# A Flamingo block's last stage: values of all head pairs two at a time, the second slot in another order

## The chip, the cores and the metric

The kernel runs on one core of a Trainium2 chip. The metric is the device time of one execution in microseconds (us). The kernel before takes 1775.0 us (median of 3 runs, 1774.93 to 1775.4). All data are float32. The core has five engines with a queue of instructions each: TensorE (PE in the profile; its weight loads are PEld), VectorE (DVE), ScalarE (ACT), GpSimd (POOL) and SyncE (SP), which here only issues DMAs. Every queue runs in order.

## The reference

Two layers of "gated cross attention, then feed forward" over 16 sequences of 256 tokens with 256 features. The change touches only the last of the four parts, a gated linear attention (GLA) with 8 heads of 64:

```python
q1 = (x @ Wq).reshape(B, L, H, DK) * scale          # keys and queries of the dense half
k1 = (x @ Wk).reshape(B, L, H, DK)
v = (x @ Wv).reshape(B, L, H, DV)
q2 = (x @ Wqa @ Wqb).reshape(B, L, H, DK) * scale    # of the sparse half
k2 = softmax((x @ Wka @ Wkb).reshape(B, L, H, DK))
gk1 = log_sigmoid(x @ Wg1a @ Wg1b + bg1) / 16        # decays
gk2 = log_sigmoid(x @ Wg2a @ Wg2b + bg2) / 16
e = softmax(x @ We);  idx = top_k(e, 1)              # each token chooses one of 4 experts
...
o = o_dense + o_sparse                               # chunked GLA, 64 tokens a chunk
g = (x @ Wga @ Wgb).reshape(B, L, H, DV)
o = o * rsqrt(mean(o * o) + EPS) * norm_w
o = o * (g * sigmoid(g))
return o.reshape(B, L, H * DV) @ Wo
```

Here `x` is the layer norm of the stream, and the result times tanh of a gate is added to the stream.

## The kernel before, in words

`stage3_fast` is the last stage. A batch is one sequence of 256 tokens, and its 8 heads are taken as 4 head pairs. Head pair p (0 to 63) belongs to batch b = p // 4, and m = p % 4 is its place in the batch. The loop `for p in range(last - 1)` runs one **slot** per head pair; a slot's number in the text is p % 4. In slot p the keys, queries and decays of head pair p+1 are made, the products of head pair p, and values of earlier head pairs.

The order of the work is written out by hand. Every instruction of this stage is tied to its place in the program, on every engine (`Pinned`, `keep_in_program_order`). The tables `middle`, `rest`, `late`, `behind_factors`, `by_rows` and `logs` give for each slot number the pieces of per-batch work to run at that point; an entry `(f, d, ...)` calls `f` for batch b + d. Waits come from the data and from buffers that are used again.

The pieces that matter here, with their names and lines:

- `keys_queries` (1861) fills one bank of PSUM, `kq`; `decays` (1869) fills `gq` and `gz` and lets ScalarE make four exponentials, `ee`; `second` (1881) puts the sparse half's queries and keys ahead into the other halves of `gq` and `gz`. `factors` (1915) multiplies `kq` by `ee` on VectorE and so frees `kq`; `factors_second` (1922) makes `k` on GpSimd and `q` on VectorE.
- `products(p, n)` (1930) makes the score products, `sc<-f` for the dense half (n = 0) and `sc<-q,k` for the sparse half (n = 1). `masked(p, n)` (1949) multiplies them by masks on VectorE, and for n = 1 GpSimd adds the two halves (`at<-at,at`).
- `values(p)` (1967) multiplies the sum by v, into the bank `o`, two head pairs to a bank. `squares` (1982 ff.) and `gated` (1991) read that bank. `summed(p)` (2110) decides which values come in which slot: both head pairs 2 and 3 of the batch before in slot 0, head pair 0 in slot 1, head pair 1 in slot 2, none in slot 3.
- `norms` (2014) makes the sums of squares (`ms`), takes them through Ln and Exp, and sends them over DRAM (`rms`, `r`) to all partitions; `normed_out` (2030) applies them on GpSimd; `project` (2035) multiplies by Wo, adds to the stream and sends out.
- `stats` (1678), `norm_ahead` (1688) and `turn_ahead` (1701) prepare the layer norm of the batch two ahead: moments on VectorE and GpSimd, the normed rows `xn` on ScalarE, and then the turn. The turn is a VectorE transpose in blocks of 32 (`turned<-xn`) and 16 DMAs on SP's queue that put the blocks into `xnT`. `bias` adds a vector to the stream ahead of stats.
- `lows` (1711) reads all of `xnT` in slot 0, for the batch one ahead. `route_logits`, `route_sums` and `route` (1735 to 1764) choose the expert; the choice goes through DRAM (`picks`) back as `rows` and `cols`. `same` (1799) and `weights` (1806) turn these into the masks `em` and `am`.
- `all_gates` (1775) makes the decays' gates: four matmuls into `sc` (two) and two rotating banks (one each), and exponentials into `lg`; the fourth exponential is put off to `gates_end`. `gate_logs` and `steepest` follow. `outgates`, `outgates_copy` and `outgates_end` (1824 to 1852) make the output gate `gw`.

PSUM has eight banks: `kq`, `gq`, `gz` and `o` one each, `sc` two, and two that rotate (`bank`).

The lines that order the values before the change:

```python
                if p % 4 == 3 and p < last - 1:
                    return
                if p % 4 == 0:
                    values(p - 2)
                values(p - 1)
                if p % 2 == 0:
                    squares((p - 1) // 4, (p - 1) % 4 // 2)
```

Of the kernel before, what the change touches and what calls it, by code (L numbers as in the profile page):

```python
# [10 lines left out]
F32 = mybir.dt.float32  # L11
I32 = mybir.dt.int32
AF = mybir.ActivationFunctionType
# [4 lines left out]
P = 128  # L18
# [55 lines left out]
def layers(ctx: ExitStack, tc: tile.TileContext, t, out, check):  # L74
# [1559 lines left out]
    def stage3_fast(early_bank):  # L1634

        with ExitStack() as sx:
# [64 lines left out]
            def turn_ahead(b):  # L1701
# [5 lines left out]
                for q in range(0, P, 32):  # L1707
                    for r in range(0, P, 32):
                        sp.dma_start(out=to[r:r + 32, :, q:q + 32], in_=y[q:q + 32, :, r:r + 32])

            def lows(b):

                low[b] = of(b).tile([P, 2, S], F32, tag="low", name="low")
                ps = bank("low")
                for c in range(2):
                    for k in range(2):
                        matmul(ps[:, c * S:(c + 1) * S], la[:, k, c * P:(c + 1) * P], xnT[b][:, k, :],
                                         start=k == 0, stop=k == 1)
# [30 lines left out]
            def route(b):  # L1749

                e, q = e_.pop(b), small("eq", few)
                w, c = choice[own_rows, :8], choice[own_rows, 8:16]
                dve.tensor_tensor(e, e, bc(den_.pop(b), few, 2), ALU.mult)
                dve.tensor_reduce(w, e, AX.X, ALU.max)
                dve.tensor_tensor(q, e, bc(w, few, 2), ALU.is_equal)
                dve.tensor_tensor(q, q, bc(prio[own_rows, 4:], few, 1), ALU.mult)
                dve.tensor_reduce(c, q, AX.X, ALU.max)
                dve.transpose(chosen[own_rows], choice[own_rows])
                sp.dma_start(out=picks[b].rearrange("n (k a) -> (n k) a", a=32), in_=chosen[64:80])
                x = w2.tile([P, 512], F32, tag="zs", name="rows") if b else w0.tile([P, 4, P], F32, tag="turned", name="rows").rearrange("p x d -> p (x d)")  # L1760
                rows[b] = x.rearrange("p (n s) -> p n s", n=2)
                sp.dma_start(out=rows[b], in_=bc(picks[b], [P, 2, S], 0))
                cols_[b] = w1.tile([P, 2, 2], F32, tag="cols", name="cols")
                sp.dma_start(out=cols_[b], in_=picks[b].rearrange("n (i p) -> p n i", p=P))
# [10 lines left out]
            def all_gates(b):  # L1775

                lg[b] = of(b).tile([P, 2, 2, 512], F32, tag="lg", name="lg")
                two = psa.tile([P, 2, 512], F32, tag="sc", name="sc")
                one = [bank("z"), bank("z")]
                for i in (1, 0):  # L1780
                    for n, (lo, hi) in enumerate(((0, 17), (32, 49))):
                        x, w = (low2[lo:hi, :], lbg2[lo:hi, :]) if i else (low[b][64 + lo:64 + hi, 1, tokens(0)],
                                                                         lbg[64 + lo:64 + hi, :])
                        matmul(two[:, n, :] if i else one[n], x, w, start=True, stop=True)
                act3.activation(lg[b][:, 0, 0, :], one[0], AF.Exp, scale=-1.0)
                act3.activation(lg[b][:, 1], two, AF.Exp, scale=-1.0)
                z_[b, "z"] = one[1]

            def gates_end(b):
                act3.activation(lg[b][:, 0, 1, :], z_.pop((b, "z")), AF.Exp, scale=-1.0)  # L1790

            def gate_logs(b, i):
                act3.activation(lg[b][:, i], lg[b][:, i], AF.Ln, bias=1.0)
# [136 lines left out]
            def products(p, n):  # L1930

                b, m, cols = place(p)
                q, k = fq.pop((p, n)), fk.pop((p, n))
                if p == last - 1 and n == 1:
                    two = [psu.tile([P, 512], F32, tag=x, name="sc1") for x in ("kq", "gq")]
                elif n == 1 and m > 1:
                    two = [bank("sc1"), bank("sc1")]
                else:
                    ps = z_[p, n, "sc"] = psa.tile([P, 2, 512], F32, tag="sc", name="sc")
                    two = [ps[:, 0, :], ps[:, 1, :]]  # L1940
                for lo, hi, i in ((0, S, 0), (P, S, 1)):
                    for j in range(2):
                        r = slice(64 * j, 64 * j + 64)
                        matmul(two[j][:, lo + i * P:hi + i * P], k[r, tokens(i)], q[r, lo:hi],
                                         start=True, stop=True)
                if n == 1:
                    z_[p, n, "sc"] = two

            def masked(p, n):
# [6 lines left out]
                else:  # L1956
# [5 lines left out]
                    if p == last - 1:  # L1962
                        at[p, 1] = a
                        return
                    pool3.tensor_tensor(at[p], at[p], a, ALU.add)

            def values(p, first=True, end=True):
                b, m, cols = place(p)
# [38 lines left out]

            rms = [tc.dram_tile([8, S], F32, name=f"rms{b}") for b in range(B - 1)]

            def scaled_first(b):  # L2010
                if b == B - 1:
                    scaled(b, 0)

            def norms(b):

                if b == B - 1:
                    return
                ps, x = bank("ms"), sq.pop(b)
                for m in range(4):
                    matmul(ps[32 * m:32 * m + 32, :S], halves[:, 48:80], x[:, m, :], start=True, stop=True)  # L2020
                y = w2.tile([P, S], F32, tag="rs", name="rs")
# [29 lines left out]
            def project_part(b, i, h):  # L2051
# [4 lines left out]
                if h == 1:  # L2056
# [4 lines left out]
            start = {}  # L2061
# [18 lines left out]
            yield  # L2080
            for group in (((stats, 0),), ((norm, 0),), ((turn, 0),), ((lows, 0),), ((gates, 0, 0), (route_logits, 0)),
                          ((route_sums, 0), (route, 0)), ((gates, 0, 1), (gate_logs, 0, 0)),
                          ((vals, 0), (gate_logs, 0, 1), (stats, 1), (steepest, 0, 0), (same, 0))):
                for f, *a in group:
                    f(*a)
                yield
# [21 lines left out]

            dve3.tensor_scalar(wo, wo3, vec[:, V_NW:V_NW + 1], None, ALU.mult)
            def summed(p):  # L2110
                if p % 4 == 3 and p < last - 1:
                    return
                if p % 4 == 0:
                    values(p - 2)
                values(p - 1)
                if p % 2 == 0:
                    squares((p - 1) // 4, (p - 1) % 4 // 2)

            for p in range(last - 1):
                run(start, p)  # L2120
# [36 lines left out]
            masked(p, 1)  # L2157
            scaled(b, 0)
            project(b - 1, 0)
            summed(p)  # L2160
            values(p, end=False)
            values(p, first=False)
            ends = Verdict()
# [138 lines left out]
```

## Time and profile before

| what | value |
|---|---|
| median of the runs | 1775.0 us (1774.93 to 1775.4) |
| profiled execution, whole | 1775.26 us |
| its span, first to last instruction | 1773.5 us |
| mean granted TensorE clock | 0.999 |
| last stage's matmuls | from 1217 us to the end |
| one batch of the last stage, 1425.10 to 1459.41 | 34.31 us: PE busy 34.31, DVE 27.07, ACT 18.96, POOL 17.72 |

In the rows of the profile a name such as `o<-at,v 128*64 128x256 f32 x16` reads: what is written, what is read, the part of TensorE's array that is used (rows*columns), the shape, the type, and how many instructions stand in the row. A timeline row begins with the start and the length of the row in us; "[0.70 <-...]" is the idle time of the engine before it, and what ended that. In the table of waits the three numbers are the total in us, how often, and the longest. Every logical float32 matmul appears as two instructions.

### The profile page before, as it was taken

Reading aid. Unit: us, or ns where it says so; the run is one execution under the profiler, and the core shown is the slowest. Engines: PE = TensorE matmul, PEld = TensorE weight load, DVE = VectorE, ACT = ScalarE, POOL = GpSimd, SP = SyncE. Lnnn points to the kernel's source line nnn. Section 1 sums busy time; section 2 is a strip of 40 time slices with the busy share of each in tenths; the row PEclk is TensorE's granted clock in tenths of the full one; section 3 lists DMA queues with packets and bytes.
Section 4 is the critical chain, followed back from the end, with each engine's and each line's share of the span. In section 5 each row is a group of like instructions: output and inputs, shape, how many; then the busy total and the mean of one; then the engine's idle time right before and its main releaser. Section 6 shows DMA issues by size and latency. Waiting matters only on the chain.

```text
span 1773.5 us, 35324 instructions
## 1 busy us (share of the span) xinstructions
PE 1753.7 (99%) x13800; PEld 1224.6 (69%) x13800; DVE 1182.6 (67%) x2713; ACT 854.6 (48%) x1764; POOL 1016.4 (57%) x1002
## 2 busy tenths in 40 slices
PE   8999999999999999999999999999999999999998
PEld 5666666666666766666678776666777777777776
DVE  3345665656566656666557358888878877877875
ACT  4434444334433443344333357886546545655653
POOL 3655676677557666677562586632544545554553
PEclk9999999999999999999999999999999999999999
DMA  9800010100100010001018883300111211211121
GB/s 309 242 1 22 14 39 7 32 20 13 32 26 20 12 36 10 29 10 35 10 56 256 248 206 49 50 14 17 32 42 36 52 42 35 51 40 42 39 45 33
DMA packets 121626, 102.31 MB, mean 58 GB/s; under 512 B 53052, under 2 KB 106980, under 8 KB 120938
## 3 DMA queue, kind: packets, MB, share of 16 engines
q1 hardware_dynamic: 109161, 83.17, 16.5%
q0 software_dynamic: 12288, 16.79, 4.7%
q8 instruction: 111, 1.82, 0.4%
q14 instruction: 66, 0.53, 0.1%
HBM read 56.26 MB, written 38.44 MB: 53 GB/s over the span
## 4 chain that ended last, share of the span: by engine, by line
PE 87%; POOL 7%; DVE 3%; issue 1%; ACT 1%; DMA 1%; SPq 0%; POOLq 0%; ACTq 0%
PE o L50 12%; PE qk L50 11%; PE v L50 9%; PE sc L50 8%; PE proj L50 8%; PE kq L1652 7%; PE sc L1652 6%; POOL es L50 4%; PE gq L1652 4%; PE v L1652 3%; PE ex L50 3%; PE proj L1652 3%; PE o L1652 3%; PE gz L1652 2%; PE q L50 2%; POOL rs L50 2%
## 5 line engine op out<-in xcount | busy, mean ns | idle before, releaser
L50 POOL TENSOR_SCALAR rs<-mv 128x2 f32<-128x2 f32 (+2 forms) x85 | 16.2, 190 | 373.1 <-DVE mv L50 366.9
L50 DVE RECIPROCAL rd<-o 128x256 f32<-128x256 f32 x64 | 112.3, 1755 | 164.2 <-PE o L50 123.8
L50 POOL TENSOR_TENSOR at<-at,at 128x768 f32<-128x768 f32 x63 | 114.3, 1814 | 144.9 <-DVE at L50 144.5
L50 ACT ACTIVATE e<-sc 128x1024 f32<-128x1024 f32 (+1 forms) x192 | 181.5, 1015 | 18.5 <-PE sc L50 18.5
L50 PE MATMUL sc<-qk 64*128 64x256 f32 (+1 forms) x1536 | 183.1, 384 | 0.5 <-DVE qk L50 0.5
L50 PE MATMUL o<-e,v 128*32 128x256 f32 (+1 forms) x3072 | 177.9, 379 | 0.0
L50 PEld LDWEIGHTS sc<-qk 64*128 64x128 f32 (+1 forms) x1536 | 132.0, 172 | 55.1 <-issue 26.8
L50 POOL TENSOR_TENSOR esum<-esum,es 128x512 f32<-128x512 f32 x128 | 163.4, 1277 | 10.0
L50 PE MATMUL qk<-kvT,wkv 128*128 128x333 f32 x512 | 164.3, 443 | 0.0
L50 ACT ACTIVATE qk<-qk 128x256 f32<-128x256 f32 x128 | 48.7, 381 | 231.8 <-PE qk L50 231.8
L50 POOL TENSOR_TENSOR es<-e 128x1024 f32<-128x1024 f32 x64 | 151.3, 2364 | 12.0 <-ACT e L50 9.0
L50 POOL TENSOR_TENSOR es<-es,e 77x1024 f32<-77x1024 f32 x64 | 150.3, 2349 | 5.0
L50 PEld LDWEIGHTS o<-e,v 128*32 128x32 f32 (+1 forms) x3072 | 99.9, 110 | 66.3
L50 PE MATMUL qk<-kvT,wq 128*128 128x256 f32 x512 | 134.6, 385 | 0.0
L50 DVE COPY qk<-qk 128x333 f32<-128x333 f32 x128 | 64.6, 504 | 93.8 <-ACT qk L50 92.8
L50 POOL DMA_INDIRECT x<-rows_out,pos x64 | 100.8, 1575 | 33.5 <-issue 15.9
L50 PEld LDWEIGHTS qk<-kvT,wq 128*128 128x128 f32 x512 | 94.2, 189 | 35.2 <-issue 9.6
L50 PEld LDWEIGHTS qk<-kvT,wkv 128*128 128x128 f32 x512 | 97.2, 190 | 30.0
L50 PE MATMUL proj<-wo0h,oT 128*128 128x256 f32 x512 | 113.7, 380 | 0.3 <-DVE oT L50 0.3
L50 PE MATMUL v<-wkv,kvT 128*128 128x512 f32 x256 | 113.1, 595 | 0.0
L50 PEld LDWEIGHTS proj<-wo0h,oT 128*128 128x128 f32 x512 | 95.9, 190 | 13.9 <-issue 0.8
L50 POOL DMA_INDIRECT rows<-xw,pos x64 | 66.7, 1041 | 57.5 <-DMA rows<-xw,pos 21.6
(256 smaller groups left out, 3912.6 us busy)
## 6 DMA issues: line engine op xcount, KB each, us to landing
rows<-zero SPq DMA_DIRECT2D x16, 640.0 KB
xin<-rows SPq DMA_DIRECT2D x16, 640.0 KB
r<-rms SPq DMA_DIRECT2D x30, 256.0 KB
rows_out<-y SPq DMA_DIRECT2D x16, 384.0 KB
v<-vctx SPq DMA_DIRECT2D x15, 308.0 KB
x<-in_x_dram SPq DMA_DIRECT2D x16, 256.0 KB
rows_out<-y SPq DMA_DIRECT2D x16, 256.0 KB
rows<-picks SPq DMA_DIRECT2D x16, 256.0 KB
```

Source lines behind the costliest of these rows:

```text
L50: x = getattr(self.engine, name)(*a, **k)
L1652: tc.keep_in_program_order(nc.tensor.matmul(*a, **k))
```

## The change

- `summed` now gives values in slots 0 and 2 only, two head pairs each time. Slot 1 has none, and its second products (n = 1) come directly behind the first, in the two rotating banks; the sum of head pair 0's halves (`both`) is put to the end of slot 1.
- The factors of the next head pair come ahead of the products in slots 1 and 62 too.
- `all_gates` makes its last exponential at once; `gates_end` goes. `norms` writes into the bank `o`.
- `outgates_end` moves from slot 1 to slot 2, `stats` from slot 1 to slot 0, `norm_ahead` from slot 2 to slot 0, `bias` from slot 0 to slot 3 of the batch before, the first `steepest` from slot 2 to slot 3.
- The turn stands behind `weights` in slot 2, except that for batch 2 it stays at the earlier place.
- `rows` lies in the tile `turned` of the first pool instead of a `zs` buffer (for batch 1 in an `sq` buffer).
- `start`, `scaled_first` and the tests for `ahead` go; the first two had no work to do.

```diff
+            def turn_in_first(b):
+                if b == 2:
+                    turn_ahead(b)
+
+            def turn_behind_first(b):
+                if b > 2:
+                    turn_ahead(b)
...
-                x = w2.tile([P, 512], F32, tag="zs", name="rows") if b else w0.tile([P, 4, P], F32, tag="turned", name="rows").rearrange("p x d -> p (x d)")
-                rows[b] = x.rearrange("p (n s) -> p n s", n=2)
+                if b == 1:
+                    rows[b] = w2.tile([P, 4, S], F32, tag="sq", name="rows")[:, :2, :]
+                else:
+                    x = w0.tile([P, 4, P], F32, tag="turned", name="rows")
+                    rows[b] = x.rearrange("p x d -> p (x d)").rearrange("p (n s) -> p n s", n=2)
...
-                z_[b, "z"] = one[1]
-
-            def gates_end(b):
-                act3.activation(lg[b][:, 0, 1, :], z_.pop((b, "z")), AF.Exp, scale=-1.0)
+                act3.activation(lg[b][:, 0, 1, :], one[1], AF.Exp, scale=-1.0)
...
-                elif n == 1 and m > 1:
+                elif n == 1 and m > 0:
                     two = [bank("sc1"), bank("sc1")]
...
-                    pool3.tensor_tensor(at[p], at[p], a, ALU.add)
+                    if m > 0:
+                        both(p, a)
+                    else:
+                        z_[p, "a"] = a
+
+            def both(p, a):
+                pool3.tensor_tensor(at[p], at[p], a, ALU.add)
...
-                ps, x = bank("ms"), sq.pop(b)
+                ps, x = psu.tile([P, 512], F32, tag="o", name="ms"), sq.pop(b)
...
-            middle = {0: [(lows, 1)], 1: [(outgates_end, 0, 0), (all_gates, 1)], 3: [(scaled_first, 0)]}
-
-            rest = {0: [(bias, 2)], 1: [(route_sums, 1), (route, 1)],
-                    2: [(norm_ahead, 2), (steepest, 1, 0)], 3: [(steepest, 1, 1)]}
-            late = {0: [(shares, 0)], 1: [(norms, -1)], 2: [(vals, 1), (turn_ahead, 2)], 3: [(project, -1)]}
-            behind_factors = {0: [(shares_end, 0)], 2: [(same, 1), (weights, 1)]}
-            by_rows = {0: [(outgates, 0), (route_logits, 1)], 1: [(gates_end, 1)]}
-            logs = {0: [(outgates_copy, 0)],
-                    1: [(stats, 2), (outgates_end, 0, 1), (gate_logs, 1, 0)],
+            middle = {0: [(stats, 2), (lows, 1)], 1: [(all_gates, 1)], 2: [(outgates_end, 0, 0)]}
+
+            rest = {1: [(route_sums, 1), (route, 1)], 3: [(gated, 0, 0), (steepest, 1, 0), (bias, 3)]}
+            late = {0: [(shares, 0)], 1: [(norms, -1)], 2: [(vals, 1), (outgates_end, 0, 1), (turn_in_first, 2)],
+                    3: [(steepest, 1, 1), (project, -1)]}
+            behind_factors = {0: [(norm_ahead, 2), (shares_end, 0)], 2: [(same, 1), (weights, 1), (turn_behind_first, 2)]}
+            by_rows = {0: [(outgates, 0), (route_logits, 1)]}
+            logs = {0: [(outgates_copy, 0)], 1: [(gate_logs, 1, 0)],
                     2: [(gate_logs, 1, 1), (normed_out, -1, 0), (normed_out, -1, 1)]}
...
-                if p % 4 == 3 and p < last - 1:
-                    return
-                if p % 4 == 0:
+                if p % 2 == 0:
                     values(p - 2)
-                values(p - 1)
-                if p % 2 == 0:
+                    values(p - 1)
                     squares((p - 1) // 4, (p - 1) % 4 // 2)
...
-                if 1 < p and p % 2 == 1:
-                    gated((p - 2) // 4, (p - 2) % 4 // 2)
+                if 1 < p and p % 4 == 1:
+                    gated(p // 4 - 1, 1)
...
-                ahead = p % 4 != 1 and p != last - 2
-                if ahead:
-                    if p % 4 < 3:
-                        factors(p + 1)
-                    run(behind_factors, p)
-                    if 0 < p:
-                        summed(p)
+                if p % 4 < 3:
+                    factors(p + 1)
+                run(behind_factors, p)
+                if 0 < p:
+                    summed(p)
                 products(p, 0)
                 masked(p, 0)
-                if not ahead:
-                    factors(p + 1)
                 run(by_rows, p)
-                if not ahead:
-                    summed(p)
+                if p % 4 == 1:
+                    products(p, 1)
                 second(p + 1)
                 factors_second(p + 1)
+                if p % 4 == 1:
+                    both(p - 1, z_.pop((p - 1, "a")))
                 run(logs, p)
-                products(p, 1)
+                if p % 4 != 1:
+                    products(p, 1)
```

More of the change, by code (lines that the diff above doesn't have):

```diff
@@ L2008, in stage3_fast @@
             rms = [tc.dram_tile([8, S], F32, name=f"rms{b}") for b in range(B - 1)]
-            def scaled_first(b):
-                if b == B - 1:
-                    scaled(b, 0)
             def norms(b):
@@ L2059, in project_part @@
                     sp.dma_start(out=out[b, tokens(i)], in_=xs[b][:, i, :])
-            start = {}
-            middle = {0: [(lows, 1)], 1: [(outgates_end, 0, 0), (all_gates, 1)], 3: [(scaled_first, 0)]}
-            rest = {0: [(bias, 2)], 1: [(route_sums, 1), (route, 1)],
-                    2: [(norm_ahead, 2), (steepest, 1, 0)], 3: [(steepest, 1, 1)]}
-            late = {0: [(shares, 0)], 1: [(norms, -1)], 2: [(vals, 1), (turn_ahead, 2)], 3: [(project, -1)]}
-            behind_factors = {0: [(shares_end, 0)], 2: [(same, 1), (weights, 1)]}
-            by_rows = {0: [(outgates, 0), (route_logits, 1)], 1: [(gates_end, 1)]}
-            logs = {0: [(outgates_copy, 0)],
-                    1: [(stats, 2), (outgates_end, 0, 1), (gate_logs, 1, 0)],
+            middle = {0: [(stats, 2), (lows, 1)], 1: [(all_gates, 1)], 2: [(outgates_end, 0, 0)]}
[5 more added lines that the diff above has]
+            logs = {0: [(outgates_copy, 0)], 1: [(gate_logs, 1, 0)],
                     2: [(gate_logs, 1, 1), (normed_out, -1, 0), (normed_out, -1, 1)]}
@@ L2082, in stage3_fast @@
                           ((route_sums, 0), (route, 0)), ((gates, 0, 1), (gate_logs, 0, 0)),
-                          ((vals, 0), (gate_logs, 0, 1), (stats, 1), (steepest, 0, 0), (same, 0))):
+                          ((vals, 0), (gate_logs, 0, 1), (stats, 1), (bias, 2), (steepest, 0, 0), (same, 0))):
                 for f, *a in group:
@@ L2110, in summed @@
             def summed(p):
-                if p % 4 == 3 and p < last - 1:
-                    return
-                if p % 4 == 0:
+                if p % 2 == 0:
                     values(p - 2)
-                values(p - 1)
-                if p % 2 == 0:
+                    values(p - 1)
                     squares((p - 1) // 4, (p - 1) % 4 // 2)
             for p in range(last - 1):
-                run(start, p)
                 if 0 < p:
                     masked(p - 1, 1)
-                if 1 < p and p % 2 == 1:
-                    gated((p - 2) // 4, (p - 2) % 4 // 2)
+                if 1 < p and p % 4 == 1:
+                    gated(p // 4 - 1, 1)
                 keys_queries(p + 1)
@@ L2159, in stage3_fast @@
             project(b - 1, 0)
-            summed(p)
+            values(p - 1)
             values(p, end=False)
```

## The prediction

> **What bounds the kernel now.** I read the page first, for the share of each engine.
>
> ```profile
> span 1773.5 us, 35324 instructions
> PE 1753.7 (99%) x13800; PEld 1224.6 (69%) x13800; DVE 1182.6 (67%) x2713; ACT 854.6 (48%) x1764; POOL 1016.4 (57%) x1002
> ```
>
> TensorE is busy 99% of the span at full clock. Next the waits of TensorE inside the last stage (1217 to 1773 us), where every edit lies:
>
> ```profile
> PE low L1652 <- issue: 0.7, 1, 0.7
> PE sc L1652 <- ACT lg L50: 0.6, 1, 0.6
> ```
>
> Two waits in 556 us: the stage lasts as long as TensorE's stream. Only two things can move its end: a shorter stream, or a new wait in it. So I read the stream by order of time, in the batch whose slot 0 opens at 1425.10 (slots 0 to 3 are the batch's four head pairs; I write c for time since that opening; the next batch opens at c 34.31).
>
> ```profile
> 1430.21 1.52 PE L1652 MATMUL o<-at,v 128*64 128x256 f32 x16
> 1431.66 0.92 PE L1652 MATMUL sc<-f 64*128 64x256 f32 x8
> 1432.41 0.38 PE L1652 MATMUL zg<-low,lbg 64*128 64x256 f32 x1
> ...
> 1439.27 0.92 PE L1652 MATMUL sc<-f 64*128 64x256 f32 x8
> 1440.12 0.87 PE L1652 MATMUL o<-at,v 128*64 128x256 f32 x8
> 1440.92 0.48 PE L1652 MATMUL gq<-low,lbk 64*128 64x256 f32 x1
> ...
> 1441.46 0.82 PE L1652 MATMUL sc<-q,k 64*128 64x256 f32 x8
> ...
> 1448.46 0.87 PE L1652 MATMUL o<-at,v 128*64 128x256 f32 x8
> 1449.26 0.92 PE L1652 MATMUL sc<-f 64*128 64x256 f32 x8
> 1450.02 0.38 PE L1652 MATMUL gq<-low,lbk 64*128 64x256 f32 x1
> ...
> 1450.45 0.82 PE L1652 MATMUL sc<-q,k 64*128 64x256 f32 x8
> ```
>
> Compare starts. Two head pairs of values together take 1.45 us (1430.21 to 1431.66), one alone 0.80 (1448.46 to 1449.26): the second costs 0.65. The lone one in slot 1 (1440.12) also stretches its neighbours: the products ahead of it take 0.85, against 0.75 where zg, of their own shape, follows; the gq/gz group behind it 0.54, against 0.43.
>
> **The gain: values two at a time.** Slot 1 loses 0.80 + 0.10 + 0.11 = 1.01 us, slot 2 gains 0.65: 0.36 per batch, 16 batches, 5.8 us. In the slot at 1748 us factors and values now also come ahead of the products, so one of its shape changes goes: 0.2. The Trainium skill (TensorEngine Tiling (Array Packing), Key Properties) says that a change of tiling mode drains the engine, with no price there; its TensorE: Matmul & The Clock Gate (Single matmul latency) gives 166 ns of constant per warm matmul. Two changes fewer would by that estimate be 0.33 a batch, 5.3 us; I take the rows' 5.8.
>
> **The turn for batch 2** (turn_in_first) keeps its place, but stats and norm_ahead come two slots earlier, so it no longer waits for xn. In the old trace that turn is what low waited for:
>
> ```profile
> 1243.00 10.83 SPq L50 DMA_DIRECT2D xnT<-turned  x16
> ```
>
> ```profile
> 1255.28 1.10 PE L1652 MATMUL low<-xnT,la 128*128 128x256 f32 x4 [0.70 <-issue]
> ```
>
> (One row each from SyncE's and TensorE's timelines.) Against other batches, where low starts at c 1.83, this one started at 2.70: 0.87 late. The transpose moves up by about 2 us, so the whole 0.87 goes. Gain in sum: 5.8 + 0.2 + 0.87 = 6.9 us.
>
> **The price: the turn of batches 3 to 15.** The turn is one VectorE transpose and 16 DMAs on SP, each held about 0.64 us by the queue; the next batch's low needs all 16. The last issue ended at 1253.83 in the pair above and low began at 1255.28: 1.45 us from last issue to low. Over 13 groups the 16 issues took 10.3 to 11.6 us, mean 10.92 (the long ones hold one issue of 0.9 to 1.8 us; in one case a 16 KB packet of the page's instruction queue lies right there). Today the transpose ends at c 21.50, so low could start at 21.50 + 0.12 + 10.92 + 1.45 = 33.99; it is due at 34.31 + 1.83 = 36.14. The spare is 2.15 us. The new place uses it up, along this chain:
>
> ```profile
> 1437.70 0.60 ACT L50 ACTIVATE lg<-z 128x512 f32<-128x512 f32 x1 [0.18 <-PE z L1652]
> 1438.20 1.02 ACT L50 ACTIVATE lg<-sc 128x1024 f32<-128x1024 f32 x1
> ```
>
> ScalarE: the first gate Exp still starts at c 12.61; with the third now directly behind (0.49 + 0.90 + 0.49) the four ee start at 14.50, one each 0.26. The ms Ln, read and Exp (0.96), the e2 Exp (0.28), the gate Ln (0.95) and, new here, outgates_end's Ln and Exp (0.65 + 0.54) end at 18.93; then slot 2's first two ee, done at 19.57. VectorE: factors(2) at 15.20, masked 15.80, q 16.68, second masked 17.01 to 18.40; it waits for ee and starts factors(3) at 19.61, then em at 20.19. GpSimd: the sum for head pair 1 (1.82) 18.54 to 20.36, then the gate product (1.28, moved here from slot 1) to 21.65.
>
> ```profile
> 1445.88 0.71 DVE L50 STREAM_TRANSPOSE turned<-xn 128x512 f32<-128x512 f32 x1 [0.41 <-ACT xn L50]
> ...
> 1447.09 1.52 DVE L50 SCALAR_TENSOR_TENSOR em<-rows,cols,dmask 128x128 f32<-128x128 f32 x2
> ...
> 1449.44 0.35 DVE L50 SCALAR_TENSOR_TENSOR am<-rows,cols 128x128 f32<-128x128 f32 x1
> ```
>
> The two em took 0.8 each, where an am of the same size took 0.35. In the trace each em ends 0.15 after a GpSimd operation (sum to 1447.73, k to 1448.46). The skill (SBUF — State Buffer, SBUF: two separate sides) says so: a VectorE operation with two SBUF inputs and a GpSimd operation exclude each other for a whole instruction. This speaks against the change, because the operation behind the sum is now 1.28 instead of 0.73. By the free row (0.35, next start after 0.26) the transpose would end at 23.1; by the lock the first em ends at 20.51, the second at 21.80, four am take 1.5, and the transpose runs 23.27 to 23.98. The first em has only 0.17 to slip in before the gate product; if it misses, 24.24. I take the middle, 24.11. Behind em stand am, the transpose and masked(2); the products for that masked end at 24.57, so nothing else is late.
>
> Low is then possible at 24.11 + 0.12 + 10.92 + 1.45 = 36.60; TensorE wants it at 36.14 - 0.36 = 35.78. The wait is 0.82 us a batch, in front of TensorE's whole queue, for 13 batches: 10.7 us. Bounds: with 23.1 only the six longest groups would make it wait (their 16 issues over 11.1 us), 1.3 us in all; 0.5 us more delay gives 17.2 us.
>
> **What costs nothing, and its cover.** SP's order is picks, rows, cols, rms, r, turn: picks leave at c 13.4 instead of 14.9, since the route's two products no longer lie under GpSimd work (0.96 and 0.99 against 0.18); rows and cols land by 19.6 (2.8 and 3.0 after issue, as now), ahead of em at 20.19; r is issued by 21.1, ahead of the turn. Behind the turn wait only the output of the batch before and slot 0's two low copies. Stats (VectorE 0.9, GpSimd 1.5) lies in VectorE's 2.07 us idle before low's copies, and on GpSimd in bias's old place; norm_ahead (1.0) between ee and sq on ScalarE, both idle there (1.26). Bias (1.27) and both steepest (1.21 each) go to slot 3, where GpSimd has nothing due and VectorE idles 2.37 us before proj. gated keeps its slots. The delayed sum of pair 0 ends at 18.3, values(0) come at 22.4. The products of slot 1's second half need the gate banks: third Exp done 14.6, they start 14.93; kq(3) needs factors(2): done 15.8, wanted 16.1. Those 0.3 us are thin, and a loss there is direct. ms in o's bank: o is free at 11.6, ms comes at 13.55. normed_out now queues behind the second gate product and k: 26.3 to 28.8, project's third operand at 29.3: 0.5 to spare, as before. Rows in the other tile: no queue, no time.
>
> **The sum**, against the profiled execution (span 1773.5, 1775.26 with what lies around it; median of the runs 1775.0): -6.9 + 10.7 = +3.8, so 1779.1 in the profile's terms; the median stands 0.3 lower, so 1778.8 against it. The last term is no better known than 0.3 x 13 = 4 us.
>
> **Rivals.** *The turn comes in time* (faster): em meets no GpSimd work, or ScalarE reaches ee sooner. It decides where low's wait falls below 6.9/13 = 0.53 us, which is a transpose that ends before c 23.8. For it: that is only 0.3 earlier than my step, and the xn wait (0.41) goes. Against: ScalarE's list above. Whole gain: 1768.1; with the 1.3 us of the lower bound 1769.4. *A wait in slot 1 as well* (slower): kq(3) or the products miss their 0.3 us, or SP meets two instruction packets. It also moves the transpose; 0.5 us a batch on top makes 1785.3. For it: three large Exp in a row ahead of ee. Against: every step is in the trace with its length. *Nothing shortens*: if the shape changes were not the cause of the 0.10 and 0.11, the gain is 0.15 a batch (2.4, with the first turn 3.3), low comes due 0.21 later (wait 0.61, in sum 7.9), and the result is 1779.6.
>
> **Chances.** Low's wait of 0.5 to 1.1 us: 0.47 (1775 to 1783). Turn in time: 0.32. Later still: 0.15. Nothing shortens: 0.06. Measurement can tell 0.2%, 3.6 us. Faster: 0.32, all of the second case. Same: 0.18, the lower third of the first. Slower: 0.50, the rest. The range reaches from the second case's full gain to just past the third's: 1768.2 to 1786.
>
> **What would show it.** Lone o groups gone from slot 1, slot 2 with x16, and kq to kq of slot 1 at 6.6 us instead of 7.65: right about the gain. Low with a wait on DMA of 0.5 to 1.1 us in 13 batches and none at the first: right about the price. The transpose at c 23.3: right about the chain; before 22.5: wrong, and the kernel is faster. The second em ending just behind a gw product: right about the lock. A wait at kq or sc of slot 1 would be the third case.

## The result, and the profile after

The changed kernel takes 1779.55 us (median of 11 runs, 1778.59 to 1780.62) beside 1775.05 us for the kernel before (11 runs, 1774.72 to 1775.4). The ratio is 1.0025, 95% interval 1.0016 to 1.0035: slower by a quarter of a per cent. The forecast was 1778.8 us, slower. The profiled execution took 1780.02 us at a clock of 0.999.

The head of the page, after:

```profile
span 1778.2 us, 35346 instructions
PE 1753.9 (99%) x13800; PEld 1225.2 (69%) x13800; DVE 1158.4 (65%) x2713; ACT 851.4 (48%) x1764; POOL 1015.2 (57%) x1002
```

TensorE's busy time is the same to 0.2 us, and the span is 4.7 us longer. So the difference shows as idle time of TensorE. The table of its waits in the last stage, after:

```profile
PE low L1652 <- DVE mv L50: 3.5, 5, 1.0
PE low L1652 <- DMA xnT<-turned: 1.6, 2, 1.1
PE sc L1652 <- ACT lg L50: 0.6, 1, 0.6
PE o L1652 <- POOL at L50: 0.4, 2, 0.2
```

Before, the two rows there came to 1.3 us. Now `low` waits in front of the whole queue: by the starts of `low` against the 1.83 us into the slot that it has without a wait, ten of the 13 batches wait, 6.6 us in all. In five of the waits the profile names an operation of VectorE (`mv`) that was long done; experiment 1 shows that it was the turn in these as well.

The waits tell only what a trace puts down as idle. The lengths of the slots, from one first key product (`kq<-xnT,wk`) to the next, tell all of it. Summed over the stage's batches, in us against the kernel before:

| part of the stage | forecast | measured |
|---|---|---|
| slot 0, `low` of batch 2 (one slot) | -0.87 | -0.71 |
| slot 0, the other batches | +10.7 | +6.51 |
| slot 1 (15 of a full batch, one last) | 16 x -1.01 = -16.2 | 15 x -0.72 and -1.00 = -11.74 |
| slot 2 (15) | +9.75 | +9.75 |
| slot 3 | 0 | 0.00 |
| from the last key products to the end | +0.45 | +1.31 |
| first key products of the stage | 0 | -0.36 |
| sum | +3.8 | +4.76 |

The sum came within 1 us, and three of its terms did not: slot 1, the price of the turn and the end. The first of them is slot 1. TensorE's rows of one slot 1, and behind the dots of its slot 2, after (batch opened at 1497.24):

```profile
1511.35 0.92 PE L1652 MATMUL sc<-f 64*128 64x256 f32 x8
1512.10 0.82 PE L1652 MATMUL sc<-q,k 64*128 64x256 f32 x8
1512.76 0.38 PE L1652 MATMUL gq<-low,lbk 64*128 64x256 f32 x1
1512.94 0.48 PE L1652 MATMUL gz<-low,lbk 64*128 64x256 f32 x1
1512.98 0.38 PE L1652 MATMUL gq<-low,lbk 64*128 64x256 f32 x1
1513.26 0.38 PE L1652 MATMUL gz<-low,lbk 64*128 64x256 f32 x1
...
1519.82 1.52 PE L1652 MATMUL o<-at,v 128*64 128x256 f32 x16
1521.27 0.92 PE L1652 MATMUL sc<-f 64*128 64x256 f32 x8
```

The lone values are gone from slot 1, and two head pairs take 1.45 in slot 2 (1519.82 to 1521.27). The products are back to 0.75 (1511.35 to 1512.10), as the forecast had it: the shape changes are gone. But the matmuls of `gq` and `gz`, which start together in pairs elsewhere, start one after another here. The first `gz` begins at 1512.94, 0.18 behind its partner, and the next key products at 1513.57, 0.81 after the group's start. In experiment 2, where the pair starts together, that is 0.53. ScalarE's row shows why:

```profile
1511.18 0.60 ACT L50 ACTIVATE lg<-z 128x512 f32<-128x512 f32 x1
1511.65 0.68 ACT L50 ACTIVATE ee<-gq 128x256 f32<-128x256 f32 x2
1512.18 0.71 ACT L50 ACTIVATE ee<-gz 128x256 f32<-128x256 f32 x2
```

The last `ee` reads the `gz` bank until 1512.89 (1512.18 + 0.71), and 0.05 later `gz` is written. The third gate exponential (1511.18), which the change put directly behind the others, is ahead of it. The table of waits does not show this wait, since TensorE's other stream (`gq`) is at work meanwhile.

### The profile page after: what moved, and what is told of

Read it like the earlier page. It is cut to its first block, busy times and chain, and to the rows that moved or that the text cites. A ratio compares the mean times of both kernels' runs of the same rounds, so it can differ in the third digit from the quotient of the medians.

```text
span 1778.2 us, 35346 instructions
## 1 busy us (share of the span) xinstructions
PE 1753.9 (99%) x13800; PEld 1225.2 (69%) x13800; DVE 1158.4 (65%) x2713; ACT 851.4 (48%) x1764; POOL 1015.2 (57%) x1002
## 4 chain that ended last, share of the span: by engine, by line
PE 85%; POOL 7%; DVE 3%; issue 1%; SPq 1%; ACT 1%; DMA 1%; POOLq 0%; ACTq 0%; DVEq 0%
PE o L50 12%; PE qk L50 11%; PE v L50 9%; PE sc L50 8%; PE proj L50 8%; PE kq L1652 6%; PE sc L1652 6%; POOL es L50 4%; PE ex L50 3%; PE v L1652 3%; PE gq L1652 3%; PE o L1652 3%; PE proj L1652 2%; PE gz L1652 2%; PE low L1652 2%; PE q L50 2%
## 5 line engine op out<-in xcount | busy, mean ns | idle before, releaser
L50 POOL TENSOR_SCALAR rs<-mv 128x2 f32<-128x2 f32 (+2 forms) x85 | 16.2, 190 | 341.3 <-DVE mv L50 338.3
L50 POOL TENSOR_TENSOR k<-e,ee 128x256 f32<-128x256 f32 x64 | 46.6, 729 | 127.9 <-ACT ee L50 124.0
```

The lines of the kernel that those rows point to most:

```text
L50: x = getattr(self.engine, name)(*a, **k)
```

## The experiments

Each ratio is to the kernel before as it ran beside the experiment (1774.5 to 1775.4 us).

**1. The turn alone.** In the changed kernel the turn of every batch stands at the earlier place.

```diff
-  2: [(vals, 1), (outgates_end, 0, 1), (turn_in_first, 2)]
+  2: [(vals, 1), (outgates_end, 0, 1), (turn_ahead, 2)]
...
-  2: [(same, 1), (weights, 1), (turn_behind_first, 2)]
+  2: [(same, 1), (weights, 1)]
```

> The changed kernel (1779.55 us) with every batch's turn at the early place, ahead of the factors, instead of behind the weights. In the changed kernel's trace low starts 0 to 1.3 us late in batches 3 to 15, 6.6 us in all. If the late turn is what low waits for, those 6.6 us go and the time is about 1772.9 us, 2.1 below the kernel before; low starts at c 1.83 in every batch. If low waits for something else (its PSUM bank, or VectorE's moments, which stand ahead of low's copies now), the time stays at 1779.5. Slot 1 stays at 6.93 us by either.

It took 1772.8 us, ratio to before 0.999 (0.9983 to 0.9996), 6.75 us less than the changed kernel (7.3 by the spans of the two profiled executions, 1770.9 and 1778.2); slot 1 stayed at 6.93, slot 0 fell to 9.40. The table of waits, of this kernel:

```profile
PE sc L1652 <- ACT lg L50: 0.6, 1, 0.6
PE o L1652 <- POOL at L50: 0.4, 2, 0.2
```

All these waits of `low` are gone, those put down to `mv` too. So the later turn is what makes the changed kernel slower than the kernel before; with the turn early the rest of the change makes it faster, though only by 0.1%.

**2. The third gate's exponential out of ScalarE's way.** VectorE copies the bank into `lg` behind the choice of the expert, and so frees it early; ScalarE takes the exponential later, in place.

```diff
-                act3.activation(lg[b][:, 0, 1, :], one[1], AF.Exp, scale=-1.0)
+                z_[b, "z"] = one[1]
+
+            def gates_copy(b):
+                dve3.tensor_copy(lg[b][:, 0, 1, :], z_.pop((b, "z")))
+
+            def gates_end(b):
+                act3.activation(lg[b][:, 0, 1, :], lg[b][:, 0, 1, :], AF.Exp, scale=-1.0)
...
-  rest = {1: [(route_sums, 1), (route, 1)], ...
+  rest = {1: [(route_sums, 1), (route, 1), (gates_copy, 1)], ...
...
-  by_rows = {0: [(outgates, 0), (route_logits, 1)]}
+  by_rows = {0: [(outgates, 0), (route_logits, 1)], 1: [(gates_end, 1)]}
```

> The changed kernel with the third gate exponential taken from ScalarE's way in slot 1: VectorE copies that bank out behind the route, and ScalarE makes the exponential in place after the norms. In the changed kernel's trace slot 1 takes 6.93 us where I had 6.64: gz of second starts 0.18 late, when ScalarE's last ee out of the same bank ends, and the pairs of gq and gz fall out of step. If that wait is the cause, slot 1 becomes 6.64 us (15 batches, 4.3 us). But the turn's chain over ScalarE and VectorE is as long as before, so low should take back what slot 1 gives wherever it waits already: 1778 to 1779. If waits in different slots just add, 1775.2. If the shape changes cost less than I read from the rows, slot 1 stays at 6.93.

It took 1773.34 us, ratio 0.9992 (0.9984 to 1.0001). Slot 1 went to 6.65, as expected: the wait at the `gz` bank was ScalarE's. Of the waits of `low` I expected the opposite of what came: they did not grow, they shrank from 6.6 to about 3.9 us. The rows of VectorE and GpSimd in slot 2 tell a part of why. First the changed kernel (batch opened at 1497.24):

```profile
1517.41 1.26 POOL L50 TENSOR_TENSOR gw<-zs,eg 128x512 f32<-128x512 f32 x1
```

```profile
1514.17 1.38 DVE L50 SCALAR_TENSOR_TENSOR at<-sc,kden,am 128x256 f32<-128x256 f32 x4
1516.90 0.69 DVE L50 TENSOR_TENSOR f<-kq,ee 128x512 f32<-128x512 f32 x1 [1.35 <-ACT ee L50]
1517.51 1.57 DVE L50 SCALAR_TENSOR_TENSOR em<-rows,cols,dmask 128x128 f32<-128x128 f32 x2
...
1520.57 0.70 DVE L50 STREAM_TRANSPOSE turned<-xn 128x512 f32<-128x512 f32 x1
```

and the kernel of this experiment (batch opened at 1492.63):

```profile
1512.43 1.26 POOL L50 TENSOR_TENSOR gw<-zs,eg 128x512 f32<-128x512 f32 x1
```

```profile
1509.19 1.38 DVE L50 SCALAR_TENSOR_TENSOR at<-sc,kden,am 128x256 f32<-128x256 f32 x4
1512.32 0.69 DVE L50 TENSOR_TENSOR f<-kq,ee 128x512 f32<-128x512 f32 x1 [1.75 <-ACT ee L50]
1512.93 1.17 DVE L50 SCALAR_TENSOR_TENSOR em<-rows,cols,dmask 128x128 f32<-128x128 f32 x2
...
1515.59 0.70 DVE L50 STREAM_TRANSPOSE turned<-xn 128x512 f32<-128x512 f32 x1
```

`em` starts at nearly the same point of the batch in both (20.27 and 20.30 us after its opening), because ScalarE's list up to it is as long. Yet the transpose ends at 24.03 in the one and at 23.66 in the other. What moved is in slot 1: with the exponential out of the way ScalarE gives `ee` sooner there, and VectorE's `factors` start at 14.64 instead of 15.13. Then the second `masked` starts at 16.56 instead of 16.93, so GpSimd's sum behind it, and the gate product behind that, end 0.37 earlier, and the first `em` ends with the gate product. The last link of the chain to the turn is GpSimd's list, which starts at that second `masked`, and not ScalarE's list up to the `ee` of slot 2. By the latter a shorter slot 1 could only bring `low` due earlier, and that was my expectation.

This is not the whole 2.7 us. A batch without a wait is 0.28 shorter too (33.90 for 34.18), so `low` is due earlier by that, and the transpose gains only 0.09 against it: 0.9 us in the ten batches that waited. Another 1.6 us come from shorter rows of 16 issues in this execution (10.64 us on average for 10.77). Such a difference needs no edit: two executions of the kernel of experiment 3 had 10.72 and 10.76, and single groups that differed by up to 0.4.

**3. Both.**

> Both: the turn early and the third gate exponential out of the way. If the two waits are all that the change lost, the time is 1779.55 - 6.6 - 4.3 = 1768.6 us, slot 1 at 6.64 us, low at c 1.83, and the gain of two values at a time stands clear. If slot 1's missing 0.29 is not ScalarE's wait, 1772.9.

It took 1768.74 us, ratio 0.9966 (0.9952 to 0.9979), which is faster than both kernels. Slot 0 is 9.40, slot 1 6.65 and slot 2 9.64: 0.42 per batch less than before, of which 0.07 is in slot 0. Slots 1 and 2 alone give -1.00 and +0.65, the 0.35 of the forecast's rows (0.36). Where the 0.07 come from was not looked into. It ran once more as the partner of number 8 below:

> The early turn with the copied gate once more, as the partner of the kernel above on the same chip: 1768.7 as in its first run, within 0.7, and a ratio to the kernel before of 0.9966 within 0.001.

There it took 1769.43 us beside 1775.23, 0.9967 (0.9955 to 0.9979).

**4. The later turn put into the kernel before**, for batches 3 to 15, and nothing else.

```diff
-  2: [(vals, 1), (turn_ahead, 2)], 3: [(project, -1)]}
+  2: [(vals, 1), (turn_in_first, 2)], 3: [(project, -1)]}
-  behind_factors = {0: [(shares_end, 0)], 2: [(same, 1), (weights, 1)]}
+  behind_factors = {0: [(shares_end, 0)], 2: [(same, 1), (weights, 1), (turn_behind_first, 2)]}
```

> The kernel before with one part of the change alone: the turn of batches 3 to 15 behind the weights, all else as it was. By the chain of the prediction: factors(3) at c 21.3, em meets the sum and k on GpSimd, the transpose ends at about 25.7 instead of 21.5; low possible at 25.7 + 0.12 + 10.92 + 1.45 = 38.2, due at 36.14: 2.05 us in each of 13 batches, 26.7 us, 1801.8. If the DMAs of the turn overlap more than that, or low needs only part of them, less than half of it, below 1788.

It took 1801.51 us, ratio 1.0152 (1.0138 to 1.0166). Its waits:

```profile
PE low L1652 <- DMA xnT<-turned: 19.3, 11, 2.7
PE low L1652 <- issue: 3.9, 3, 1.8
PE sc L1652 <- ACT lg L50: 0.6, 1, 0.6
```

The sum came out to 0.3 us of the expected 1801.8, but in part by chance. The starts of `low` are 24.6 us late in all, where 26.7 were expected. Another 1.7 us were lost in one slot 0, where the granted clock of TensorE was 0.50 from 1475.09 to 1478.50, 0.4 us after an idle time of 2.14 us, and the matmuls of `low` came 0.43 us apart instead of 0.21. A longer idle time elsewhere in this run, 2.7 us, was not followed by it, and no other run here has a lower clock before the last 10 us of its span. From the transpose's end on, the price of a turn can be estimated before it is moved, from 16 issues and 1.45 us. The difference to the changed kernel comes from the moves around the turn: here the transpose ends 8.62 us before the next batch opens, there 10.14 before it.

**5. The values ahead of the products in slot 1 of the kernel before**, to price the shape changes alone.

```diff
-                ahead = p % 4 != 1 and p != last - 2
+                ahead = p != last - 2
```

> The kernel before (1774.7 us in the last runs) with one thing changed: in slot 1 the factors and the lone values come ahead of the products, so that one change of the array's shape fewer stands in the slot; the same matmuls, no turn or ScalarE work moved. If a change of shape costs what I read from the rows, the block norms, values, products, second loses about 0.23 us against norms, products, values, second: 16 batches, 3.7 us, about 1771.0, and slot 1 goes from 7.65 to 7.42. If the shape changes cost nothing, no change.

A miss: 1786.01 us, ratio 1.006 (1.0047 to 1.0074). The part that was meant to be priced is as expected (slot 1, this kernel):

```profile
1443.22 0.87 PE L1652 MATMUL o<-at,v 128*64 128x256 f32 x8
1444.03 0.92 PE L1652 MATMUL sc<-f 64*128 64x256 f32 x8
1444.78 0.38 PE L1652 MATMUL gq<-low,lbk 64*128 64x256 f32 x1
1444.79 0.38 PE L1652 MATMUL gz<-low,lbk 64*128 64x256 f32 x1
1445.00 0.38 PE L1652 MATMUL gq<-low,lbk 64*128 64x256 f32 x1
1445.01 0.38 PE L1652 MATMUL gz<-low,lbk 64*128 64x256 f32 x1
1446.08 0.92 PE L1652 MATMUL sc<-q,k 64*128 64x256 f32 x8 [0.70 <-DVE at L50]
```

The products take 0.75 instead of 0.85 and the group behind them 0.43 instead of 0.54 (1444.78 to 1445.21, where the next would start). So the 0.10 and 0.11 belong to the place of the lone values, between the products and that group. What I left out is the last row: 0.70 us of waiting in every batch (11.0 us in the table of waits). The second products need the `sc` bank that the first mask has to free, and that mask now comes 0.8 later. The changed kernel doesn't have this wait, as its second products in slot 1 go to the rotating banks.

**6. No GpSimd work under the masks.** In the changed kernel VectorE makes each batch's first gate product itself, behind the turn.

```diff
-                pool3.tensor_tensor(gw[b][:, h::2, :], ...)
+                if h == 1:
+                    pool3.tensor_tensor(gw[b][:, h::2, :], ...)
+                else:
+                    z_[b, "first"] = zs, e
...
+            def outgates_first(b):
+                zs, e = z_.pop((b, "first"))
+                dve3.tensor_tensor(gw[b][:, 0::2, :], ...)
...
-  2: [(same, 1), (weights, 1), (turn_behind_first, 2)]
+  2: [(same, 1), (weights, 1), (turn_behind_first, 2), (outgates_first, 0)]
```

> The changed kernel (1779.55 us) with the first gate product of each batch on VectorE, behind the turn, in place of GpSimd: the operation under which em lies is gone. If the lock is what holds em (1.3 us instead of 0.35 in the changed kernel's trace), both em take 0.35, the transpose ends near c 23.1 instead of 24.0, and low's waits of 6.6 us shrink to about 0.5: 1773.4. If em waits for its rows and cols from DRAM instead, em and the time stay as they are.

It took 1775.12 us, ratio 0.9999 (0.999 to 1.0008), 1.7 more than expected. VectorE's rows, of this kernel (batch opened at 1493.08):

```profile
1512.74 0.69 DVE L50 TENSOR_TENSOR f<-kq,ee 128x512 f32<-128x512 f32 x1 [1.35 <-ACT ee L50]
1513.35 0.61 DVE L50 SCALAR_TENSOR_TENSOR em<-rows,cols,dmask 128x128 f32<-128x128 f32 x2
...
1515.43 0.70 DVE L50 STREAM_TRANSPOSE turned<-xn 128x512 f32<-128x512 f32 x1
```

Nothing but the engine of one product was changed, and the two `em` take 0.61 together instead of 1.57. The transpose ends at 23.05 instead of 24.03, and the waits of `low` shrink from 6.6 to 0.4 us in all. The gap to the expectation lies elsewhere. The end behind the last key products is 1.80 longer than before (0.49 more than in the changed kernel), slot 0 of the last batch but one takes 9.82 instead of 9.40, and the stage starts 0.67 later in this execution. The kernel before was slower in this comparison as well, 1775.43 for 1775.05.

**7, 8 and 10. The end.** From the last key products on, every version with the change's order takes longer. In the faster kernel of experiment 3, number 7 puts the order of the values in the last two slots back; number 8 puts the closing of the output gate of the last batch back into slot 1, so that GpSimd's gate products don't fall into the last slot; number 10 does both. The core of number 8:

```diff
-  middle = {..., 1: [(all_gates, 1)], 2: [(outgates_end, 0, 0)]}
+  middle = {..., 1: [(outgates_last, 0, 0), (all_gates, 1)], 2: [(outgates_rest, 0, 0)]}
...
+            def outgates_last(b, h):
+                if b == B - 1:
+                    outgates_end(b, h)
```

and of number 7:

```diff
-                if p % 4 < 3:
+                if p % 4 < 3 and p < last - 2:
                     factors(p + 1)
                 run(behind_factors, p)
-                if 0 < p:
+                if 0 < p < last - 3:
                     summed(p)
...
+                if p >= last - 3:
+                    summed(p)
```

> The version with both waits gone (1768.74 us), and the last two slots in the order of the kernel before: there, pairing gained 0.36 and then lost 1.7 us to waits for GpSimd's last sums (slot 61 and what follows take 32.5 us against 31.8). If that is right, 0.7 us less, 1768.0. If the end only varies from run to run, no change.

> This is the early turn with the copied gate, and in addition the last batch's closing of the gates (and so GpSimd's gate products of that batch) put back into slot 1, as before the change. If those products, which now fall into the last slot ahead of GpSimd's sums, are what makes the end after the last key products 1.3 to 1.7 us longer than before, the end shrinks from about 27.2 to about 25.9 us and the kernel takes about 1.2 us less than its partner in this call, some 1767.5. If the end is long for another reason, it takes the same as its partner, 1768.7, within 0.4. If ScalarE's list in slot 1 of the last batch grows too long, slot 1 of that batch is 0.3 us longer and the gain 0.9.

> The early turn with the copied gate, and in the last batch both the order of the values in the last two slots and the place of the output gate's closing as before the change. Each of the two alone left the last three head pairs' values at 11.3 us behind the last key products (9.85 before the change). If either cause alone is enough to hold them, both together bring them back to 9.85, the last matmul back from 19.0 to 17.55 behind the last key products, and slot 61 stays at 6.32: slot 61 and the end together 0.4 us shorter than in the early turn with the copied gate, a ratio of 0.9964 to the kernel before. If a third thing holds VectorE or GpSimd there, the values stay at 11.3 and the kernel takes what it took with the old order alone, ratio 0.9972.

Numbers 7 and 8 missed: 1770.47 (0.9972, 0.9961 to 0.9982) and 1769.54 (0.9967, beside 0.9967 of its partner). Number 10 took 1768.52 (0.9966, 0.9952 to 0.9979), no less than experiment 3 by its time. The trace tells them apart, in us after the last key products:

| kernel | slot 61 | values of the last three head pairs start | last group of matmuls starts | slot 61 and up to that group |
|---|---|---|---|---|
| before | 6.32 | 9.85 | 17.55 | 23.87 |
| after | 5.32 | 11.31 | 19.01 | 24.33 |
| 3, both | 5.32 | 11.29 | 18.99 | 24.31 |
| 7, old order | 6.32 | 11.29 | 18.99 | 25.31 |
| 8, gates back | 5.32 | 11.35 | 19.05 | 24.37 |
| 10, both back | 6.32 | 10.08 | 17.78 | 24.10 |

Either cause alone holds those values at 11.3; only with both gone do they come near 9.85. Two views show them. GpSimd's rows in number 7: the gate products and `u` fill the engine without a gap up to the last sum, which ends at 1753.20, and the values start at 1753.26.

```profile
1745.78 2.50 POOL L50 TENSOR_TENSOR gw<-zs,eg 128x512 f32<-128x512 f32 x2
1748.25 0.71 POOL L50 TENSOR_TENSOR k<-e,ee 128x256 f32<-128x256 f32 x1
1748.93 2.50 POOL L50 TENSOR_TENSOR u<-u,r 128x512 f32<-128x512 f32 x2
1751.39 1.81 POOL L50 TENSOR_TENSOR at<-at,at 128x768 f32<-128x768 f32 x1
```

TensorE's rows in number 8: the values of the last slot, which stand ahead of the products now, come earlier and wait for the sum of head pair 61, and the products with their masks wait behind them.

```profile
1743.60 0.87 PE L1652 MATMUL o<-at,v 128*64 128x256 f32 x8
1744.98 0.87 PE L1652 MATMUL o<-at,v 128*64 128x256 f32 x8 [0.51 <-POOL at L50]
```

Number 10 is 0.2 us shorter there than experiment 3 (24.10 for 24.31), half of what was expected; what holds the values 0.23 past 9.85 was not tried. What follows varies more than that: from the start of the last group to the end it took 8.18 and 7.45 us in two executions of the kernel of experiment 3.

## Why the prediction came out, step by step

**TensorE bounds the stage: right.** The difference was found in the lengths of its slots and in its end, but for 0.36 of its start.

**Values two at a time, 0.36 per batch: right in size, not reached.** Slot 2 grew by 0.65, to the digit. Slot 1 fell by 0.72, not 1.01. The failed step is "the products of slot 1's second half need the gate banks: third Exp done 14.6, they start 14.93". I followed the gate banks and not the banks `gq` and `gz` themselves, whose other halves `second` writes while ScalarE still reads `ee` out of them. The forecast's own figures hold the two times and do not compare them: four `ee` of 0.26 from 14.50 end at 15.54, and the group comes 0.75 behind 14.93, at 15.68. Measured they were 15.65 and 15.52, the wrong way round. Before, the lone values stood between and gave it 0.80 us. That cost 0.29 a batch, 4.3 us in 15. In the last batch, which has no gates of a next one to make, slot 1 did fall by 1.00. Experiment 2, which takes the third exponential out of ScalarE's list there, brings slot 1 to 6.65, and experiment 3 gives 0.35 of the rows' 0.36. The estimate from the Trainium skill's constant per matmul (TensorE: Matmul & The Clock Gate, Single matmul latency), 0.33, lies 0.02 below this 0.35; the page gives that constant for a single matmul and not for a change of shape, so that no run here tests why it comes so near.

**The first turn: right in kind.** Slot 0 of that batch fell by 0.71 instead of 0.87. That `low` still started 0.19 later than the 1.83 of the others. The turn's last issue had ended 3.27 us before, and no `low` that waited for a turn started more than 2.23 behind one, so it was hardly the turn's doing; the start at 2.02 is the same in experiments 1, 2, 3 and 6, and what it waited for was not tried.

**The price of the turn: right in kind, too large.** Its parts: the transpose ended at 24.03 (forecast 24.11). The 16 issues took 10.77 us on average (10.92). `low` was due 0.23 later than I had it, since a batch without a wait is 34.18 us long and not 33.95. Against these, from the last issue to `low` it took 1.67 us on average in the groups that waited, where I had the 1.45 of a single pair. For the ten batches that waited, whose 16 issues took 10.89 on average, this gives 24.03 + 0.07 + 10.89 + 1.67 = 36.66 against a due time of 34.18 + 1.83 = 36.01: 0.65 us ten times. By the starts of `low` it is 6.6 us in all, 0.51 a batch over 13, for 0.82 and 10.7. The table has 6.51 because slot 0 without a wait is 0.07 shorter than before and a slot with one loses 0.08 more than the wait. The forecast's own sign, a wait of 0.5 to 1.1 us in 13 batches, was met in five of them. The groups fall in two: those with 16 even issues (10.34) and those that hold a long one. Two of them, after, SP's rows; the first was followed by `low` with a wait of 1.13, the second by `low` in time:

```profile
1345.90 11.40 SPq L50 DMA_DIRECT2D xnT<-turned  x16
...
1521.34 10.34 SPq L50 DMA_DIRECT2D xnT<-turned  x16
```

The mean hides this: three batches had no wait, one had 1.28. In each of the seven groups with a long issue, after, a 16 KB packet of the instruction queue (q8 in the profile's list of DMA queues) runs during that issue, and in the six even groups none begins; before, nine groups of the 13 have such a packet and the long issue with it. This goes beyond the one case of the prediction, but no run moved the packets, so that the cause is not shown.

One reading of the kernel before holds only in part, and did no harm. In four of its 13 batches the turn did not start at the transpose's end at 21.50, since the two issues of `r` came late and stood ahead of it in SP's queue. In the batch of the prediction's rows,

```profile
1446.41 1.33 SPq L50 DMA_DIRECT2D r<-rms  x2
1447.85 11.55 SPq L50 DMA_DIRECT2D xnT<-turned  x16
```

the turn began at 22.75 and ended at 34.31, and with 1.45 behind it 0.38 us were to spare, not 2.15. After the change `r` is issued before the transpose ends in every batch, as forecast.

**The lock between VectorE and GpSimd: right.** The first `em` missed its 0.17 us: the two start at 1517.51, GpSimd's gate product ends at 1518.67, and the next operation starts at 1519.01, one free `em` (0.35) behind it. So it was the first that ended just behind the gate product, and not the second. Experiment 6 shows the lock: without the product both run free. By the forecast's figures that case ends the transpose at 24.24; the gate product ended at 21.43 instead of 21.65, and that makes 24.02. So 24.03 lies near the middle that I took, 24.11, through an early gate product. Where I went wrong is expectation 2, which followed ScalarE's list alone: the forecast's chain already ended on GpSimd's product, and experiment 2 showed that its start, the sum behind the second `masked` of slot 1, decides.

**The end, +0.45: too small by 0.86.** For the slot at 1748 us I counted the shape change that goes (0.2), and neither that its values, put ahead of the products, wait for GpSimd's sum, nor that the gate products had moved into GpSimd's last slots (numbers 7, 8 and 10).

**The sum.** Slot 1 (+4.4), the end (+0.9) and the first turn (+0.2) added to the forecast; the smaller price of the turn (-4.2) and an earlier start of the stage (-0.4) took away. The start is variation between executions: the experiments have it between 1217.0 and 1218.3. That slot 1 and the turn cancel is in part no chance: the wait in slot 1 delays the moment at which `low` is due, and leaves the chain to the turn where it was, so 0.23 us a batch is waited only once, by estimate 2.3 us in the ten batches that waited. The rest of the 4.2 is luck: it comes from the turn's other parts, which have nothing to do with slot 1. The rival "a wait in slot 1 as well" had named this slot and a wait there, at the wrong bank and with 0.5 us a batch on top; it did occur, with 0.29, and in place of part of the wait of `low`.

## What to carry to other kernels

When work between two steps on the bounding engine is taken away, look up for each buffer that the later step writes who read it last, the other half of the same bank too: the removed work may have been the cover. When a transfer is moved later, add up its whole chain from the engine that ends last to the landing, and read the landing from several groups; with a spare of some tenths in ten us, count it as lost. Take such a change apart before judging it: with the turn left early and one gate bank copied out, its pairs of values make the kernel 0.34% faster, where the whole made it 0.25% slower.

## What was not expected of the hardware

- A wait of 0.18 us at one of two streams that run side by side on 64 rows of the array each (`gz` beside `gq`) cost 0.29 us. The two stayed out of step until the next full-array matmul (`kq`).
- The 16 issues of the turn take 10.33 or 10.34 us in six groups in a row, and up to 11.44 in others of the same execution, where one issue takes 0.78 to 1.66 us instead of 0.64, each time with a 16 KB packet of the instruction queue beside it.
- From a turn's last issue to the `low` that waited for it, 1.45 to 2.23 us passed within one execution. Most of this is no scatter: nine of the ten times came back within 0.03 us in experiment 4. Batches 3 to 8 had 1.45, 1.54, 1.64, 1.73, 1.60 and 1.49 us in the changed kernel, and 1.48, 1.55, 1.65, 1.72, 1.60 and 1.49 there. What sets the sequence is open.
- In experiment 4 the granted clock fell to 0.50 for 3.4 us in the middle of the stage, behind an idle time of 2.14 us of TensorE; it cost 1.7 us.
